# Reordering the end of a gated cross-attention and feed-forward kernel: who casts the last pair but one, and where its last addition stands

## The chip, the cores and the metric

The kernel runs on one core of one Trainium2 chip. The metric is the device time of one execution in microseconds (us), as the median over several timed runs. A profiled execution is a separate run of the same program with the hardware profiler on. A core has five engines that work side by side, each through its own list of instructions in order: TensorE (PE in the profile; PEld is its weight load), VectorE (DVE), ScalarE (ACT), GpSimd (POOL) and SyncE (SP), which issues DMAs.

## The reference

There are 16 sequences of 224 tokens with 512 features (3584 tokens) and, for each, 750 context rows with 384 features under a mask. Cut to what matters:

```python
def act_quant(x):
    scale = 127.0 / clip(max(abs(x), axis=-1), 1e-05)
    return clip(round(x * scale), -128, 127) / scale

def bitlinear(x, w, b):                 # w is rounded to -1, 0, 1 times a scale
    return act_quant(rmsnorm(x)) @ weight_quant(w).T + b

x = x + tanh(g_xattn) * cross_attention(layernorm(x), context, mask)   # 8 heads of 64
h = bitlinear(layernorm(x), w1, b1)     # 512 -> 2048
h = gelu(h)
x = x + tanh(g_ffn) * bitlinear(h, w2, b2)   # 2048 -> 512
```

The rounding of `act_quant` needs the greatest absolute value of a whole row first. So in the feed-forward part each row of `h` is finished, its maximum is taken, the row is scaled and rounded, transposed, and only then multiplied by `w2`.

## The kernel before, in words

The tokens are cut into 28 tiles of 128 rows; two tiles are a *pair*, 14 pairs, numbered 0 to 13, and a tile is row 0 or row 1 of its pair. "Row 12/1" below is the second tile of pair 12. The attention of one sequence after another runs on all engines, and the feed-forward work of the pairs is woven into it (`merge`). The changed lines belong to the end, where attention is over and only pairs 11, 12 and 13 are left.

What one row goes through in the feed-forward part:

- `project` multiplies the attention output by `wo` (TensorE, L1252) and VectorE adds it to the residual `y` (L1255). `normalise` makes the quantised `xq` of it on VectorE (L1290 to L1300) and, on POOL, the factor `c1`. The last pair's `xq` is transposed by TensorE in `turn_rows` (L1321) and copied out by ScalarE (L1322).
- `up`, or `up_last` for pair 13, multiplies by `w1` (L1333, L1411); VectorE evicts the product to `h` (L1341, L1419), ScalarE applies gelu (L1366, L1758, L1422). The last pair is evicted in halves; its rows live in the tiles named `h_last` (row 0) and `xoT` (row 1).
- The maximum of the row on VectorE: `a`, L1369, in `gelu`; for pair 13 the maxima of the halves, `am`, L1423, in `up_last`, and their combination, L1434, in `gelu_last`.
- The quantiser on VectorE (L1264, L1265), the rounding to 16-bit integers (L1372; L1441 for pair 13) and the cast of the integers to bf16, in place, in the tile `hq`. VectorE casts at L1375 for all pairs up to 11 and at L1442 for pair 13. For pair 12 ScalarE casts, in two halves, at L1379.
- The transposition of `hq` into `hqT`: by a DMA that SP issues (L1382), or, for rows 12/1, 13/0 and 13/1, in `turn_by_tensor` by TensorE (L1354) with ScalarE's copies (L1355).
- `down` multiplies by `w2`: 16 products into one accumulator (L1472). `down` can run something between its eighth and ninth product.
- `mean_square` sums squares on ScalarE (L1451), and POOL makes the factor `c2` in `measure_last` or `gelu` (L1272 to L1274).
- `store` adds the product, times `c2`, to `y` on VectorE (L1485), and POOL issues the indirect DMA that scatters the rows to the output (L1487).

The order of instructions on each engine is not the program's order: a scheduler lays out each engine's list before the run. `tc.issue_after(x)` tells it that what is written inside must stand behind `x`; an engine then works through its list strictly in turn, so an instruction that waits holds up all behind it. `late["rounded"]` remembers the last cast of a row by VectorE, and the end uses it as such an anchor. The end of the program, from the last up products on, reads before the change:

```python
    mean_square(i, 1)
    added, sent = store(i - 1, 1)
    gelu_last(i, 0)
    with tc.issue_after(added):
        gelu_last(i, 1)
```

Here i is 13: row 12/1 is added and sent, and both roundings of the last pair follow.

Of the kernel before, what the change touches and what calls it, by code (L numbers as in the profile page):

```python
# [11 lines left out]
ALU = mybir.AluOpType  # L12
AX = mybir.AxisListType
# [157 lines left out]
def flamingo_gated_kernel(  # L171
# [74 lines left out]

    stages = []
    compact = compact_path(ctx, tc, sh, x, context, out, late_loads, stages)
    next(compact)
    n_odd = nc.values_load(sh.n_odd[0:1, 0:1], min_val=0, max_val=2 * x.shape[0])  # L250
# [484 lines left out]
def compact_path(ctx, tc, sh, x, context, out, late_loads, stages):  # L735
# [3 lines left out]
    nc = tc.nc  # L739
# [3 lines left out]
    FF = sh.FF  # L743
# [12 lines left out]
    I16 = mybir.dt.int16  # L756
# [29 lines left out]
    def wide(shape, dtype, name):  # L786
        return ps_sim.tile(shape, dtype, tag="sim", name=name)
# [6 lines left out]
    def pow_half(dst):  # L794
        nc.gpsimd.tensor_tensor(dst, dst, sh.mhalf[:, : dst.shape[1]], ALU.pow)

    def small(name, n=2):
        return pa.tile([P, n], F32, tag=f"s{n}", name=name, bufs=24 if n == 2 else 6)


    def token(t):
        return sh.token[:, t // 7, t % 7 : t % 7 + 1]
# [433 lines left out]
    late = {}  # L1236
# [25 lines left out]
    def quantiser(amax, part, least, name):  # L1262
        k = small(f"k_{name}")
        nc.vector.tensor_scalar(k[:, part], amax[:, part], least, 1.0 / 127.0, ALU.max, ALU.mult)  # L1264
        nc.vector.reciprocal(k[:, part], k[:, part])  # L1265
        load["v"] += 300
        return k

    def unquantiser(amax, r, part, isw, name):

        c = small(f"c_{name}")
        nc.gpsimd.tensor_tensor(c[:, part], amax[:, part], r[:, part], ALU.mult)  # L1272
        nc.gpsimd.tensor_scalar(c[:, part], c[:, part], 1e-5, None, ALU.max)
        latest["p"] = nc.gpsimd.tensor_scalar(c[:, part], c[:, part], isw, None, ALU.mult).ins  # L1274
        return c
# [82 lines left out]
    def gelu(i, ks=(0, 1)):  # L1358
        f = pairs[i]
        name = f"{i}_{ks[0]}"  # L1360
        part = slice(ks[0], ks[-1] + 1)
        ss = small(f"ss_{name}")
        amax = small(f"a2_{name}")
        for k in ks:
            if (i, k) != (NPAIR - 2, 1):
                nc.scalar.activation(f["h", k], f["h", k], AF.Gelu)  # L1366
        for k in ks:
            h = f["h", k]
            nc.vector.tensor_reduce(amax[:, k : k + 1], h, AX.X, ALU.max, apply_absolute_value=True)  # L1369
            scale = quantiser(amax, slice(k, k + 1), 1e-5 * EPS**0.5, f"2_{i}_{k}")  # L1370
            hq = late["rows"].tile([P, FF], BF16, tag="hq", name=f"hq_{i}_{k}", bufs=3)
            nc.vector.tensor_scalar(hq.bitcast(I16), h, scale[:, k : k + 1], None, ALU.mult)  # L1372
            f["hqT", k] = hqT = late["rows"].tile([P, NF, P], BF16, tag="hqT", name=f"hqT_{i}_{k}", bufs=2)
            if i < NPAIR - 2:
                late["rounded"] = nc.vector.tensor_copy(hq, hq.bitcast(I16)).ins  # L1375
            else:
                for g in range(2):
                    cols = slice(g * FF // 2, (g + 1) * FF // 2)
                    nc.scalar.copy(hq[:, cols], hq.bitcast(I16)[:, cols])  # L1379
            f["hq", k] = hq  # L1380
            if (i, k) != (NPAIR - 2, 1):
                nc.sync.dma_start_transpose(out=hqT, in_=hq)  # L1382
        if (i, ks[0]) == (NPAIR - 2, 1):
            f["a2", 1] = amax[:, 1:2]
            return
        for k in ks:
            nc.scalar.activation(f["h", k], f["h", k], AF.Square, accum_out=ss[:, k : k + 1])  # L1387
        r = small(f"r2_{name}")
        nc.gpsimd.tensor_scalar(r[:, part], ss[:, part], 1.0 / FF, EPS, ALU.mult, ALU.add)
        pow_half(r[:, part])  # L1390
        c = unquantiser(amax, r, part, sh.isw[1], f"2_{name}")
        for k in ks:
            f["c2", k] = c[:, k : k + 1]
        load["v"] += len(ks) * (2282 + 1280 + 690)
        load["s"] += len(ks) * 2 * 1910 + 2600

    def up_last(i, k):

        f = pairs[i]
        if k == 0:  # L1400
            place = pa.tile([P, 12, S], F32, tag="pT", name="h_last", bufs=1)
            h = place.rearrange("p n q -> p (n q)")[:, :FF]
        else:
            h = xoT.rearrange("p n q -> p (n q)")[:, :FF]
        most = small(f"am_{i}_{k}")
        for g in range(2):
            ph = wide([P, 2, NB], F32, f"hp_{i}_{k}_{g}")
            for n in range(2):
                at = (2 * g + n) * NB
                for d in range(ND):  # L1410
                    last = nc.tensor.matmul(  # L1411
                        ph[:, n, :],
                        lhsT=f["xqT"][:, k * ND + d, :],
                        rhs=w1T[:, d, at : at + NB],
                        start=(d == 0),
                        stop=(d == ND - 1),
                    )
            cols = slice(2 * g * NB, 2 * (g + 1) * NB)
            nc.vector.scalar_tensor_tensor(  # L1419
                h[:, cols], ph.rearrange("t i n -> t (i n)"), f["c1", k], sh.b1[:, cols], ALU.mult, ALU.add  # L1420
            )
            nc.scalar.activation(h[:, cols], h[:, cols], AF.Gelu)  # L1422
            nc.vector.tensor_reduce(most[:, g : g + 1], h[:, cols], AX.X, ALU.max, apply_absolute_value=True)  # L1423
        f["h", k], f["most", k] = h, most
        return last.ins

    def gelu_last(i, k):

        f = pairs[i]
        name = f"{i}_{k}"  # L1430
        part = slice(k, k + 1)
        h = f["h", k]
        amax = small(f"a2_{name}")
        nc.vector.tensor_reduce(amax[:, part], f["most", k], AX.X, ALU.max)  # L1434
        scale = quantiser(amax, part, 1e-5 * EPS**0.5, f"2_{name}")
        hq = late["rows"].tile([P, FF], BF16, tag="hq", name=f"hq_{name}", bufs=3)
        f["hqT", k] = hqT = late["rows"].tile([P, NF, P], BF16, tag="hqT", name=f"hqT_{name}", bufs=2)
        half = FF // 2
        for g in range(2):
            cols = slice(g * half, (g + 1) * half)  # L1440
            nc.vector.tensor_scalar(hq.bitcast(I16)[:, cols], h[:, cols], scale[:, part], None, ALU.mult)  # L1441
            nc.vector.tensor_copy(hq[:, cols], hq.bitcast(I16)[:, cols])  # L1442
        f["hq", k], f["a2", k] = hq, amax[:, part]

    def mean_square(i, k):
        f = pairs[i]
        name = f"{i}_{k}"
        squares = small(f"sq_{name}")
        for g in range(2):
            junk = pa.tile([P, 2, D], F32, tag="x", name=f"sq_{name}_{g}", bufs=3)  # L1450
            nc.scalar.activation(  # L1451
                junk.rearrange("p k d -> p (k d)"),
                f["h", k][:, 2 * g * NB : 2 * (g + 1) * NB],
                AF.Square,
                accum_out=squares[:, g : g + 1],
            )
        f["r2", k] = r = small(f"r2_{name}")
        nc.gpsimd.tensor_tensor(r[:, 0:1], squares[:, 0:1], squares[:, 1:2], ALU.add)
        nc.gpsimd.tensor_scalar(r[:, 0:1], r[:, 0:1], 1.0 / FF, EPS, ALU.mult, ALU.add)
        pow_half(r[:, 0:1])  # L1460
# [20 lines left out]
    def store(i, k):  # L1481
        f = pairs[i]
        po = f["po", k]
        y = f["y"][:, k, :]
        added = nc.vector.scalar_tensor_tensor(y, po, f["c2", k], y, ALU.mult, ALU.add)  # L1485
        load["v"] += 700
        sent = nc.gpsimd.indirect_dma_start(  # L1487
            out=out_rows,
            out_offset=bass.IndirectOffsetOnAxis(ap=token(2 * i + k), axis=0),
            in_=y,  # L1490
            in_offset=None,
            bounds_check=B * S - 1,
            oob_is_err=False,
        )
        return added.ins, sent.ins

    NPAIR = NTOK // 2

    def up_pieces(i):
        p = []  # L1500
        for k in range(2):
            p += [(1.8, lambda g=g, k=k: up(i, k, g)) for g in range(2)]
            p.append((0.0, lambda k=k: gelu(i, (k,))))
        return p
# [244 lines left out]
    i = NPAIR - 1  # L1749
# [22 lines left out]
    with tc.issue_after(lowered):  # L1772
        up_last(i, 0)
        mean_square(i, 0)
        turn_rows(i, 1)
        raised = up_last(i, 1)
# [2 lines left out]
        turn_by_tensor(i - 1, 1)  # L1779
        lowered = down(i - 1, 1)  # L1780
    mean_square(i, 1)
    added, sent = store(i - 1, 1)
    gelu_last(i, 0)
    with tc.issue_after(added):
        gelu_last(i, 1)
    with tc.issue_after(raised):
# [44 lines left out]
```

## Time and profile before

| | us |
|---|---|
| timed runs, median of 3 (lowest to highest) | 740.0 (739.37 to 740.6) |
| profiled execution, its own time | 735.04 |
| profiled execution, span of the trace | 733.0 |
| TensorE busy in the span | 676.0 (92%) |
| VectorE busy | 492.2 (67%) |
| ScalarE busy | 416.2 (57%) |
| GpSimd busy | 394.1 (54%) |

The span is what the trace covers; 2 us of the profiled execution lie around it. The engines' shares are averages over the whole run. The granted TensorE clock was 0.981 of full speed over the span. A row of a timeline gives start, length, engine, line of the code, operation, output and inputs by name, shapes, how many instructions were merged, and in brackets how long the engine had been idle before it and what released it.

### The profile page before, as it was taken

How to read it: one execution, taken by the hardware profiler on the slowest of the kernel's cores; microseconds unless marked ns; L12 is line 12 of the kernel's file. 1: busy time of each engine (PE TensorE's matmuls, PEld its weight loads, DVE VectorE, ACT ScalarE, POOL GpSimd, SP SyncE). 2: the span in 40 equal slices, each digit the busy share in tenths (PEclk: the TensorE clock that was granted, in tenths of full speed). 3: DMA queues.
4: the chain of work that ended last, by engine and by line, in shares of the span. 5: the costliest groups of instructions: out<-in, count | busy, mean ns of one | idle time of the engine just before them, and what ended most of it. 6: DMA issues, size and time to landing. Idle time of an engine off the chain costs nothing.

```text
span 733.0 us, 11422 instructions
## 1 busy us (share of the span) xinstructions
PE 676.0 (92%) x3917; PEld 432.1 (59%) x3917; DVE 492.2 (67%) x1294; ACT 416.2 (57%) x978; POOL 394.1 (54%) x549
## 2 busy tenths in 40 slices
PE   4998899999999999897999999999999999999862
PEld 3876677666555656564556665766665665544331
DVE  5586856877484775673667857839585765889760
ACT  2549555384673864646627549547373746574560
POOL 5583676464464644755447562656545453554631
PEclk9989999999999999999999999999999999999997
DMA  7884031032222232321233321123313221422200
GB/s 236 288 288 144 14 104 32 16 75 57 65 54 58 83 58 72 70 59 58 54 61 104 58 81 38 41 72 74 83 43 72 58 59 44 86 73 58 58 15 33
DMA packets 79858, 56.74 MB, mean 77 GB/s; under 512 B 68176, under 2 KB 68320, under 8 KB 79664
## 3 DMA queue, kind: packets, MB, share of 16 engines
q1 hardware_dynamic: 71728, 30.17, 17.6%
q0 software_dynamic: 8064, 25.76, 11.4%
q8 instruction: 33, 0.54, 0.3%
q14 instruction: 33, 0.27, 0.1%
HBM read 32.06 MB, written 7.34 MB: 54 GB/s over the span
## 4 chain that ended last, share of the span: by engine, by line
PE 63%; DVE 10%; issue 9%; POOL 9%; ACT 4%; DMA 3%; POOLq 0%; DVEq 0%; ACTq 0%
PE qp L1066 11%; PE op L1252 10%; PE fp L1472 8%; PE hp L1333 8%; PE kp L946 5%; PE sim L1106 4%; PE vp L962 4%; PE ptp L1163 3%; PE av L1188 2%; POOL p L1140 2%; DVE a L1369 2%; PE xnp L1045 2%; POOL x L808 2%; DMA hqT<-hq 1%; POOL out_dram L1487 1%
## 5 line engine op out<-in xcount | busy, mean ns | idle before, releaser
L1140 POOL TENSOR_TENSOR p<-p,rec 112x768 f32<-112x768 f32 (+2 forms) x64 | 79.6, 1246 | 72.0 <-DVE rec L1139 28.1
L1130 ACT ACTIVATE p<-p,nm 112x192 f32<-112x192 f32 (+2 forms) x256 | 104.8, 413 | 10.3 <-DVE nm L1120 7.3
L1472 PE MATMUL fp<-w2T,hqT 128*128 128x512 fp8e4 x448 | 102.6, 382 | 3.8 <-DMA hqT<-hq 2.2
L1066 PE MATMUL qp<-xnT,wq_sb 128*128 128x224 f32 x512 | 105.1, 359 | 0.6 <-ACT xnT L781 0.6
L1252 PE MATMUL op<-wo_sb,xoT 128*128 128x512 f32 x224 | 103.7, 599 | 0.0
L1333 PE MATMUL hp<-w1T,xqT 128*128 128x512 fp8e4 x416 | 99.3, 383 | 3.0 <-DVE nm L1120 1.4
L1066 PEld LDWEIGHTS qp<-xnT,wq_sb 128*128 128x128 f32 x512 | 97.0, 193 | 6.4 <-issue 3.1
L1341 DVE SCALAR_TENSOR_TENSOR h<-hp,c,b_bc 128x1024 f32<-128x1024 f32 x52 | 66.5, 1281 | 43.6 <-PE hp L1333 43.3
L1120 DVE CUSTOM_DVE_ANT_0 p<-sim,mask 112x192 f32<-112x192 f32 (+2 forms) x224 | 56.0, 303 | 32.5 <-PE sim L1106 31.9
L1472 PEld LDWEIGHTS <-hqT 128*128 128x128 bf16 x448 | 42.7, 98 | 58.8 <-issue 6.3
L1369 DVE TENSOR_REDUCE a<-h 128x1 f32<-128x2048 f32 x26 | 59.3, 2281 | 20.3 <-ACT h L1366 20.3
L1487 POOL DMA_INDIRECT out_dram<-y,token x28 | 32.0, 1143 | 67.2 <-DVE y L1485 62.1
L1333 PEld LDWEIGHTS <-xqT 128*128 128x128 bf16 x416 | 39.9, 98 | 47.4 <-issue 8.5
L1485 DVE SCALAR_TENSOR_TENSOR y<-fp,c,y 128x512 f32<-128x512 f32 x28 | 20.9, 746 | 68.0 <-PE fp L1472 66.4
L1252 PEld LDWEIGHTS op<-wo_sb,xoT 128*128 128x128 f32 x224 | 40.7, 190 | 38.8 <-issue 36.3
L946 PE MATMUL kp<-ctxT,wk_sb 128*128 128x192 f32 (+1 forms) x360 | 59.9, 316 | 0.0
L946 PEld LDWEIGHTS kp<-ctxT,wk_sb 128*128 128x128 f32 x360 | 54.5, 198 | 5.4 <-issue 3.8
L1387 ACT ACTIVATE h<-h 128x2048 f32<-128x2048 f32 x25 | 47.7, 1909 | 17.1 <-DVE hq L1372 11.8
L1312 POOL TENSOR_TENSOR y<-y,b_bc 128x512 f32<-128x512 f32 x28 | 37.0, 1321 | 34.6 <-DVE fx L1292 34.3
L781 ACT COPY pT<-ptp 128x448 f32<-128x448 f32 (+1 forms) x62 | 32.3, 536 | 39.9 <-PE ptp L1163 39.7
L781 ACT COPY qT<-qp 128x448 f32<-128x448 f32 x29 | 15.4, 532 | 65.7 <-PE qp L1066 65.4
L1106 PE MATMUL sim<-kT,qT 64*112 64x192 f32 (+2 forms) x512 | 50.8, 311 | 0.6 <-DVE nm L1120 0.6
(200 smaller groups left out, 1250.5 us busy)
## 6 DMA issues: line engine op xcount, KB each, us to landing
raw<-in_L_ffn_w_dram SPq DMA_DIRECT2D x16, 512.0 KB, 5.4
wq_sb<-in_L_xattn_W_q_dram SPq DMA_DIRECT2D x1, 1024.0 KB, 5.8
b_bc<-in_L_ffn_b_dram SPq DMA_DIRECT2D x1, 1024.0 KB, 8.3
wk_sb<-in_L_xattn_W_k_dram SPq DMA_DIRECT2D x1, 768.0 KB, 7.4
wv_sb<-in_L_xattn_W_v_dram SPq DMA_DIRECT2D x1, 768.0 KB, 8.8
wo_sb<-in_L_xattn_W_o_dram SPq DMA_DIRECT2D x1, 512.0 KB, 4.0
wo_sb<-in_L_xattn_W_o_dram SPq DMA_DIRECT2D x2, 256.0 KB, 6.0
y<-in_x_dram,token POOLq DMA_INDIRECT x28, 3.5
```

Source lines behind the costliest of these rows:

```text
L946: nc.tensor.matmul(pk[:, p - p0, :], lhsT=sh.wk[:, c, p * P : (p + 1) * P], rhs=st["ctxT"][:, c, :cap], start=(c == 0), stop=(c == NC - 1),)
L1066: nc.tensor.matmul(pq[:, i, :], lhsT=sh.wq[:, d, (p + i) * P : (p + i + 1) * P], rhs=st["xnT"][:, d, :], start=(d == 0), stop=(d == ND - 1),)
L1106: nc.tensor.matmul(sim[:, j, i, :cap], lhsT=st["qT"][j * DH : (j + 1) * DH, p, q * TQ : (q + 1) * TQ], rhs=keys["kT"][j * DH : (j + 1) * D ...
L1120: nc.vector.tensor_tensor_reduce(out=probs[:, h, :cap], in0=sim[:, j, i, :cap], in1=keys["mask"][:, first + j * begin : first + j * begin ...
L1130: nc.scalar.activation(probs[:, h, :cap], probs[:, h, :cap], AF.Exp, bias=nmax, scale=-1.0, accum_out=total[:TQ, h : h + 1],)
L1140: nc.gpsimd.tensor_tensor(probs[:, :, first : first + cap], probs[:, :, :cap], rec[:TQ].unsqueeze(2).to_broadcast([TQ, 4, cap]), ALU.mult,)
L1252: last = nc.tensor.matmul(po, lhsT=xoT[:, d, at : at + P], rhs=sh.wo[:, d, :], start=(d == 0), stop=(d == ND - 1))
L1333: last = nc.tensor.matmul(ph[:, n, :], lhsT=f["xqT"][:, k * ND + d, :], rhs=w1T[:, d, at : at + NB], start=(d == 0), stop=(d == ND - 1),)
L1341: nc.vector.scalar_tensor_tensor(h[:, cols], ph.rearrange("t i n -> t (i n)"), f["c1", k], sh.b1[:, cols], ALU.mult, ALU.add)
L1369: nc.vector.tensor_reduce(amax[:, k : k + 1], h, AX.X, ALU.max, apply_absolute_value=True)
L1387: nc.scalar.activation(f["h", k], f["h", k], AF.Square, accum_out=ss[:, k : k + 1])
L1472: last = nc.tensor.matmul(po, lhsT=f["hqT", k][:, n, :], rhs=w2T[:, n, :], start=(n == 0), stop=(n == NF - 1))
```

## The change

Three things are changed, all at the end. First, `gelu` casts every row on VectorE, pair 12 included, and remembers that cast as `late["rounded"]`. Second, in `up_last` the maxima of the last pair are laid behind that anchor, so the rounding and cast of row 12/1 stand in front of them on VectorE. Third, `gelu_last` returns its last cast, and `store` of row 12/1, its addition on VectorE and its scatter on POOL, is laid behind the casts of row 13/0; the rounding of row 13/1 stays behind the addition.

```diff
@@ gelu
-            if i < NPAIR - 2:
-                late["rounded"] = nc.vector.tensor_copy(hq, hq.bitcast(I16)).ins
-            else:
-                for g in range(2):
-                    cols = slice(g * FF // 2, (g + 1) * FF // 2)
-                    nc.scalar.copy(hq[:, cols], hq.bitcast(I16)[:, cols])
+            late["rounded"] = nc.vector.tensor_copy(hq, hq.bitcast(I16)).ins
             f["hq", k] = hq
@@ up_last
             nc.scalar.activation(h[:, cols], h[:, cols], AF.Gelu)
-            nc.vector.tensor_reduce(most[:, g : g + 1], h[:, cols], AX.X, ALU.max, apply_absolute_value=True)
+            with tc.issue_after(late["rounded"]):
+                nc.vector.tensor_reduce(most[:, g : g + 1], h[:, cols], AX.X, ALU.max, apply_absolute_value=True)
@@ gelu_last
             nc.vector.tensor_scalar(hq.bitcast(I16)[:, cols], h[:, cols], scale[:, part], None, ALU.mult)
-            nc.vector.tensor_copy(hq[:, cols], hq.bitcast(I16)[:, cols])
+            rounded = nc.vector.tensor_copy(hq[:, cols], hq.bitcast(I16)[:, cols])
         f["hq", k], f["a2", k] = hq, amax[:, part]
+        return rounded.ins
@@ the end
     mean_square(i, 1)
-    added, sent = store(i - 1, 1)
-    gelu_last(i, 0)
+    with tc.issue_after(gelu_last(i, 0)):
+        added, sent = store(i - 1, 1)
     with tc.issue_after(added):
         gelu_last(i, 1)
```

In the compiled order other instructions move with these. On VectorE row 13/0's reduction, scale and rounding stand ahead of row 13/1's residual addition, and the first maximum of the last pair stands behind the eviction of row 13/1's first half instead of before it. On ScalarE the gelu of row 13/1's first half stands ahead of the squares of row 13/0. On TensorE the four transposes of row 13/0's `xq` stand between the eighth and ninth product of row 12/0 instead of behind the sixteenth. On POOL one small operation trades places with its neighbour. SP's list is the same. The lines of the changed kernel after L1374 are 3 to 5 lower than those before.

## The prediction

> **What bounds the kernel now.** The busy shares come first and settle little: TensorE is busy 92% of the 733.0 us span, but the change touches only the last 60 us, so that stretch has to be read by itself. I read, in this order, the chain of waits from 640 us on, the timelines of VectorE and TensorE over the same stretch, then windows of it, and the rows of the casts.
>
> The chain (start, length, what it went through):
>
> ```profile
> 678.55 1.04 ACT hq L1379
> 679.59 0.03 ACT h L1387
> 679.61 4.57 DMA hqT<-hq
> 684.18 0.05 issue
> 684.23 3.64 PE fp L1472 x16
> ...
> 701.51 3.77 PE fp L1472 x16
> 705.28 0.03 issue
> 705.31 0.02 DVEq L1485
> 705.33 0.04 issue
> 705.37 0.75 DVE y L1485
> ```
>
> Read two things. ScalarE's second half-cast of pair 12, row 0 ends at 679.59; the transposing DMA then takes 4.57 us, and the products of that row start at 684.23, though the projection before them ended at 683.14. And later VectorE's addition y of pair 12, row 1 starts as the 16 products of that row end. After this the chain goes through POOL's small c operations to 711.24 and then shows 5.59 us of "issue"; nothing ran on POOL there, so I follow VectorE and TensorE instead (start, length, operation, in brackets the idle time before):
>
> ```profile
> 702.45 1.22 DVE L1423 TENSOR_REDUCE am<-xoT 128x1 f32<-128x1024 f32 x1 [0.63 <-ACT xoT L1422]
> 705.37 0.75 DVE L1485 SCALAR_TENSOR_TENSOR y<-fp,c,y 128x512 f32<-128x512 f32 x1 [1.71 <-PE fp L1472]
> 706.61 1.42 DVE L1441 TENSOR_SCALAR hq<-h_last,k 128x1024 int16<-128x1024 f32 x2
> 707.94 0.96 DVE L1442 CAST hq<-hq 128x1024 bf16<-128x1024 int16 x2
> ```
>
> ```profile
> 708.63 1.48 PE L1354 MATMUL hqp<-ident,hq 128*128 128x128 bf16 x16 [3.36 <-DVE hq L1442]
> 710.36 2.95 PE L1472 MATMUL fp<-w2T,hqT 128*128 128x512 fp8e4 x8 [0.25 <-ACT hqT L1355]
> 713.15 1.06 PE L1354 MATMUL hqp<-ident,hq 128*128 128x128 bf16 x16
> 714.04 5.34 PE L1472 MATMUL fp<-w2T,hqT 128*128 128x512 fp8e4 x24
> ```
>
> The last maximum ends at 703.67. The last pair's rounding needs nothing more, yet it starts at 706.61: VectorE first waits 1.71 us for the addition's products and then adds. TensorE idles 3.36 us meanwhile, and its next 8 products take 2.95 us where 16 took 3.75. The windows say why (window, its length, busy time of PE, PEld, DVE, ACT, POOL, then the granted TensorE clock, DMA share, GB/s):
>
> ```profile
> 81.02:84.43 3.41, 1.24 (x13) 1.03 (x14) 3.41 (x11) 1.26 (x5) 3.12 (x5) 1.00 0.00 0
> 695.40:698.80 3.40, 1.65 (x10) 0.58 (x8) 3.40 (x4) 3.40 (x7) 0.82 (x3) 1.00 0.00 0
> 705.66:709.07 3.41, 0.44 (x8) 0.45 (x9) 3.34 (x12) 0.00 (x0) 2.88 (x7) 1.00 0.05 18
> 709.07:712.49 3.42, 3.17 (x18) 1.53 (x16) 2.02 (x4) 1.93 (x2) 2.10 (x4) 0.51 0.17 63
> ```
>
> After a nearly empty window TensorE ran at half clock for 3.4 us. So the end is a ring of VectorE, ScalarE and TensorE in which VectorE's order decides.
>
> **The change part by part.** Times below are of the profiled execution (735.04 us, span 733.0); the timed runs have a median of 740.0 (739.37 to 740.6), 5.0 above it. I work out a difference at the end and take it off 740.0, as nothing before 677 us is changed. All places are from the compiled order of both kernels.
>
> *Step 1, row 0's cast.* Removed: two ScalarE casts (2 x 1.03 us). Added: one VectorE cast, 0.69 us, behind the addition that ends at 677.94, so done at 678.56 instead of 679.59. SP issues the same transposing DMA 1.03 earlier; with 4.57 us it lands at 683.15, when the projection (end 683.14) frees TensorE. Products start at 683.2, gain 1.0. ScalarE, 2 us freer, does its squares earlier, with slack on POOL.
>
> *Step 2, the normalisation of pair 13.* Its row 0 now goes ahead of row 1 on VectorE: reduction, scale and rounding end at 683.6, row 1's residual addition (ready at 683.14) at 684.25, row 0's cast at 684.45 instead of 687.05. So TensorE's four transposes (0.39) now stand in the middle of the 16 products (3.63), which end at 687.25; the up products follow at once (688.76 before). Row 1's chain on VectorE by its own rows (0.68, 0.18, 0.48, 0.67, 0.3, 0.48), the addition y (0.75, ready at 687.3) and the cast end at 688.45 instead of 689.91.
>
> *Step 3, VectorE is full here* (8.00 of 8.00 us in 690 to 698), so each operation counts. From 688.4: a2 of row 12/1 2.28, two h_last evictions 2 x 1.27, rounding 1.27, end 694.5; first xoT eviction to 695.7 (about 699.2 before, because one maximum, 1.2, now comes later); the moved cast 0.69 to 696.3 (ScalarE's ended at 699.61); two maxima to 698.6; second xoT eviction to 699.8; a third maximum to 701.0.
>
> *Step 4, ScalarE.* Its order is now: gelu of the first xoT half (until 696.8, it waits for the eviction at 695.7), squares 2.1 (698.85), two hqT copies (700.75; their transposes end at 697.6), gelu of the second half (701.75). Queued behind that early gelu are the squares and the copies, so TensorE's products of row 12/1 run from 699.95 to 703.7 (705.26 before). The last maximum starts at 701.8 and ends at 703.0 instead of 703.67. Six microseconds of ScalarE work stand between the first xoT eviction and this maximum, which is why 3.5 us gained there shrink to 0.65.
>
> *Step 5, the moved addition.* The rounding follows the maximum directly: with the 0.57 us of small operations it starts at 703.55 instead of 706.61, gain 3.06; without steps 1 to 4 the order alone would give 2.4 (idle 1.71 plus the addition's 0.7). Row 0's transposes start at 705.6 (708.63), its products at 707.3 (710.36). The addition now follows row 0's casts, 705.75 to 706.45, then row 1's scale (0.5) and rounding: casts end at 709.0 instead of 711.1. POOL's scatter of that row waits for the addition (until 706.45, before 706.12), and its c operations wait behind the scatter: they end near 711.5 instead of 711.24. The next addition needs its c only at 712, so that costs nothing; the cover is 0.5 to 1 us.
>
> *Step 6, the clock.* Before, 8 products ran at half clock, 2.95 us for 1.82: 1.1 us. After, TensorE's gap is about 1.9 us. The trace's row: windows with 0.44 and 1.24 us of TensorE work of 3.41 were followed by half clock, one with 1.65 was not. The Trainium skill ("TensorE: Matmul & The Clock Gate", What's actually happening) has the clock drop after an idle window of about 3.4 us; a gap of 1.9 us would then be free and the gain 3.06 + 1.1 = 4.2. By the rows, windows over the new gap, with the transposes, hold 1.3 to 1.9 us, at the edge, and the phase is unknown; if it drops, the gain is about 3.0. A half-clock stretch on the products from 699.95 would end them near 705.4, still ahead of 705.6. I take 0.6 of the 1.1, nearer to neither row.
>
> *Step 7, contention.* A rule speaks against the cast on VectorE: "SBUF — State Buffer", Who interferes with whom, has casts contend with GpSimd, where "Whoever issues first gets the shared pair for the whole instruction". The casts' rows:
>
> ```profile
> L1375 DVE CAST hq<-hq x24: 653/688/3275, 159.6 to 667.1; 128x2048 bf16<-128x2048 int16 x24
> 206.57 3.27 DVE L1375 CAST hq<-hq 128x2048 bf16<-128x2048 int16 x1
> ```
>
> One of 24 lost 2.6 us, with POOL's row operations (206.54 to 209.29) on top of it. At the new places POOL has a scatter's issue (678.23 to 679.33) and, at 695.7, nothing. By the rule a cast that loses to the scatter ends near 680 and step 1 is void; by the row of a rounding that overlapped such an issue (204.98, 1.39 us for 1.28) it costs 0.1. I take the row.
>
> Sum: 3.06 + 0.6 = 3.7 us, so 736.3.
>
> **The rivals.** *A, the early half brings nothing.* The transpose lands no earlier (it now starts beside the scatter of row 11/1, which already overlaps it) or a cast stalls; then the two casts' 1.4 us on the full VectorE eat steps 1 to 4, and step 5's 2.4 with little clock is left: about 737.5. For: landings of these DMAs range from 4.2 to 6.0 us. Against: the median is 4.3.
>
> *B, one long stall.* One of the two casts loses 2.6 us to POOL as at 206.57: 3.7 - 2.6, 738.9, within what can't be told from no change.
>
> *C, slower: both casts stall behind POOL.* Place: 677.9 and 695.7 on VectorE, with everything of the last pair queued behind. Price 2 x 2.6 = 5.2 against 3.7: 741.5. It decides once the stalls on the chain pass 3.7 us, and slower can be measured past 5.2. For: the one row. Against: POOL's timeline has no row operation at either place.
>
> *D, the order does not act as said*, or another wait takes the place of the addition's (the last maximum still held by ScalarE until after 704): 740. Against: the compiled order has the addition behind the roundings.
>
> **How the numbers follow.** This measurement can tell about 0.2%, 1.5 us, from no change. Main forecast 0.72: 736.3, by itself 735.2 to 737.2. A 0.13: 737.5. B 0.07: 738.9. C 0.05: 741.5. D 0.03: 740. Faster is the first and A, 0.85; same is B and D, 0.10; slower is C, 0.05. The range 735.1 to 738.5 takes in the first two with the clock's both ends (4.2 and 3.0) and some of the error in a chain of thirty estimated steps.
>
> **What would show it.** Right: products of row 12/0 start within 0.2 us of the projection's end; xqp transposes in the middle of them; first xoT eviction about 3.5 us earlier; last maximum only 0.3 to 1 us earlier; no idle before the rounding of the last pair, and its transposes about 3 us earlier; 8 products in 1.8 or 2.95 us tell step 6. Wrong: a cast of 128x2048 well over 0.7 us in the last 60 us; an idle gap ahead of the last maximum of more than 2 us on ScalarE's gelu; an addition y of the last pair that waits for POOL's c.

## The result, and the profile after

The changed kernel takes 736.91 us (median of 7 runs, 733.75 to 738.65) where the kernel before takes 740.6 beside it: ratio 0.9939, 95% interval 0.9915 to 0.9963. (The medians are 3.7 us apart, the means, 736.23 and 740.76, 4.5; the ratio goes with the means.) Two later comparisons of the same pair gave 0.9925 (0.9903 to 0.9946) and 0.9941 (0.9917 to 0.9964). So it is faster, by about what was forecast (736.3). But step 1 of the sum went the other way and carried the steps behind it along: nearly all that can be shown of the gain is step 5's.

Every execution reaches the end with an offset of its own: the projection of pair 13, ahead of which nothing was changed, starts at 676.11 us before, at 679.72 after, and between 676.7 and 681.6 in the other traces. That spread is larger than the effect. So places are given below as **offsets from the start of that projection** (L1252): a row's start, or its start plus its length, minus the start of the first row here. The last addition ends at offset 44.13 before and 42.57 after. The rows before, then after:

```profile
676.11 7.03 PE L1252 MATMUL op<-wo_sb,xoT 128*128 128x512 f32 x16
684.23 3.63 PE L1472 MATMUL fp<-w2T,hqT 128*128 128x512 fp8e4 x16 [1.09 <-DMA hqT<-hq]
...
719.49 0.75 DVE L1485 SCALAR_TENSOR_TENSOR y<-fp,c,y 128x512 f32<-128x512 f32 x1 [2.71 <-PE fp L1472]
```

```profile
679.72 7.03 PE L1252 MATMUL op<-wo_sb,xoT 128*128 128x512 f32 x16
...
721.54 0.75 DVE L1482 SCALAR_TENSOR_TENSOR y<-fp,c,y 128x512 f32<-128x512 f32 x1 [2.70 <-PE fp L1469]
```

VectorE's timeline of the changed kernel:

```profile
681.47 0.68 DVE L1374 CAST hq<-hq 128x2048 bf16<-128x2048 int16 x1
...
701.11 0.68 DVE L1374 CAST hq<-hq 128x2048 bf16<-128x2048 int16 x1
...
707.16 1.22 DVE L1419 TENSOR_REDUCE am<-xoT 128x1 f32<-128x1024 f32 x1 [0.79 <-ACT xoT L1417]
...
708.86 1.42 DVE L1437 TENSOR_SCALAR hq<-h_last,k 128x1024 int16<-128x1024 f32 x2
...
712.02 0.75 DVE L1482 SCALAR_TENSOR_TENSOR y<-fp,c,y 128x512 f32<-128x512 f32 x1 [1.07 <-PE fp L1469]
```

Both moved casts (L1374) take 0.68 us. The rounding of row 13/0 follows the last maximum after 0.48 us of small operations (2.94 before, with the addition between), and the addition y now stands behind it. But the maximum itself ends at 708.38, offset 28.66, where it ended at 27.56 before: 1.1 us later. TensorE's timeline says why:

```profile
689.06 1.90 PE L1469 MATMUL fp<-w2T,hqT 128*128 128x512 fp8e4 x8 [2.31 <-DMA hqT<-hq]
690.80 0.39 PE L1321 MATMUL xqp<-ident,xq 128*128 128x128 bf16 x4
...
705.32 6.59 PE L1469 MATMUL fp<-w2T,hqT 128*128 128x512 fp8e4 x16 [2.40 <-ACT hqT L1355]
711.75 1.06 PE L1354 MATMUL hqp<-ident,hq 128*128 128x128 bf16 x16
713.46 1.90 PE L1469 MATMUL fp<-w2T,hqT 128*128 128x512 fp8e4 x8 [0.66 <-ACT hqT L1355]
```

The products of row 12/0 wait 2.31 us for their transposing DMA (1.09 before). Those of row 12/1 wait 2.40 us for ScalarE's copies and then take 6.59 us for 16 where full clock needs 3.63. The chain of waits shows both:

```profile
682.22 6.80 DMA hqT<-hq
689.01 0.05 issue
689.06 1.90 PE fp L1469 x8
...
702.19 2.17 ACT sq L1448 x4
704.37 0.90 ACT hqT L1355
705.27 0.05 issue
705.32 6.61 PE fp L1469 x16
711.97 0.04 issue
712.02 0.75 DVE y L1482
```

The DMA took 6.80 us where it took 4.57 before, and two squares on ScalarE (four instructions, each square with the read of its sum) stand in front of the copies. Three windows around the 16 products (columns as before: PE busy first, granted clock after POOL):

```profile
701.31:704.73 3.42, 1.07 (x16) 0.90 (x16) 3.42 (x4) 3.42 (x6) 0.20 (x2) 0.97 0.00 0
704.73:708.14 3.41, 2.82 (x7) 1.01 (x8) 2.62 (x3) 3.41 (x6) 0.76 (x2) 0.50 0.00 0
708.14:711.56 3.42, 3.42 (x10) 1.20 (x9) 2.70 (x8) 1.06 (x3) 1.56 (x3) 0.53 0.00 0
```

The window with TensorE's gap has 1.07 us of work; half clock follows for two windows. It falls on row 12/1's products instead of the last pair's first eight, which are back at 1.90 us for 8 (2.95 before).

### The profile page after: what moved, and what is told of

The parts are those of the page before. It is cut to its first block, busy times and chain, and to the rows that moved or that the text cites. A ratio compares the mean times of both kernels' runs of the same rounds, so it can differ in the third digit from the quotient of the medians.

```text
span 735.1 us, 11419 instructions
## 1 busy us (share of the span) xinstructions
PE 678.2 (92%) x3917; PEld 433.7 (59%) x3917; DVE 490.1 (67%) x1296; ACT 413.0 (56%) x974; POOL 395.3 (54%) x549
## 4 chain that ended last, share of the span: by engine, by line
PE 58%; issue 11%; POOL 10%; DVE 8%; DMA 5%; ACT 3%; POOLq 0%; SPq 0%; ACTq 0%; DVEq 0%
PE op L1252 11%; PE qp L1066 9%; PE fp L1469 8%; PE hp L1333 8%; PE sim L1106 4%; PE kp L946 4%; PE vp L962 4%; PE ptp L1163 2%; DMA hqT<-hq 2%; DMA raw<-in_L_ffn_w_dram 2%; PE av L1188 2%; POOL p L1140 2%; POOL out_dram L1484 1%; DVE a L1369 1%; POOL x L808 1%
## 5 line engine op out<-in xcount | busy, mean ns | idle before, releaser
L1469 PE MATMUL fp<-w2T,hqT 128*128 128x512 fp8e4 x448 | 104.6, 387 | 6.5 <-DMA hqT<-hq 3.4
L1252 PE MATMUL op<-wo_sb,xoT 128*128 128x512 f32 x224 | 103.7, 599 | 0.0
L1252 PEld LDWEIGHTS op<-wo_sb,xoT 128*128 128x128 f32 x224 | 40.7, 190 | 38.8 <-issue 36.4
```

The source lines that it names most:

```text
L1252: last = nc.tensor.matmul(po, lhsT=xoT[:, d, at : at + P], rhs=sh.wo[:, d, :], start=(d == 0), stop=(d == ND - 1))
L1469: last = nc.tensor.matmul(po, lhsT=f["hqT", k][:, n, :], rhs=w2T[:, n, :], start=(n == 0), stop=(n == NF - 1))
```

## The experiments

All in one table. Ratios are timed, against the kernel before on the same chip. The other columns come from the one trace of each kernel: the wait in front of the products of row 12/0, then offsets from the projection's start, then the time from the last pair's first rounding to the end.

| kernel | ratio (95%) | wait 12/0 | last maximum ends | rounding starts | end | rounding to end |
|---|---|---|---|---|---|---|
| before | 1 | 1.09 | 27.56 | 30.50 | 44.13 | 13.63 |
| after | 0.9939 (0.9915–0.9963) | 2.31 | 28.66 | 29.14 | 42.57 | 13.43 |
| a2_after_again | 0.9925 (0.9903–0.9946) | 2.23 | 28.58 | 29.06 | 41.43 | 12.37 |
| a3_after_beside | 0.9941 (0.9917–0.9964) | 2.40 | 28.75 | 29.23 | 41.60 | 12.37 |
| e1_add_only | 0.9933 (0.9908–0.9958) | 1.08 | 27.55 | 28.04 | 42.31 | 14.27 |
| e2_add_back | 1.0025 (1.0013–1.0036) | 2.34 | 28.69 | 32.27 | 46.32 | 14.05 |
| e3_row0_scalar | 0.9941 (0.9924–0.9959) | 1.10 | 28.21 | 28.70 | 41.06 | 12.36 |
| e4_scatter_later | 0.9943 (0.9919–0.9966) | 0 | 27.49 | 27.97 | 40.33 | 12.36 |
| e4b (e4 again) | 0.9939 (0.9917–0.9961) | 0 | 27.51 | 28.00 | 40.36 | 12.36 |
| e5_squares_later | 0.9934 (0.9914–0.9955) | 2.27 | 27.81 | 28.30 | 42.31 | 14.01 |
| e6_busy | 0.9936 (0.9916–0.9957) | 2.38 | 30.23 | 30.71 | 43.07 | 12.36 |
| e7_both | 0.9927 (0.9903–0.9950) | 0 | 26.71 | 27.19 | 42.02 | 14.83 |
| e8_both_busy | 0.9919 (0.9888–0.9949) | 0 | 26.71 | 27.19 | 39.55 | 12.36 |
| e8b (e8 again) | 0.9921 (0.9892–0.9950) | 0 | 26.71 | 27.19 | 39.55 | 12.36 |

Read the last column first. From the last pair's rounding to the end it is 12.36 us in every trace in which no half-clock stretch slows this part, and 1.1 to 2.5 more where one does. The rest is where the rounding starts.

The timed ratios do not follow the traces that finely: all kernels with the moved addition lie between 0.9919 and 0.9943 with intervals that overlap, while their traces end between 39.55 and 43.07 us. So timing shows the moved addition alone (e1 and e2); what the other experiments say rests on their traces, one or two of each.

**The addition alone, and everything but the addition.** e1 is the kernel before with only the third part of the change; e2 is the changed kernel with only that part undone.

```diff
# e1, on the kernel before (gelu_last returns its last cast)
-    added, sent = store(i - 1, 1)
-    gelu_last(i, 0)
+    with tc.issue_after(gelu_last(i, 0)):
+        added, sent = store(i - 1, 1)
# e2, on the changed kernel: the reverse
```

> The kernel before with the moved addition alone: row 12/1 is added and sent behind the casts of row 13/0; casts and maxima stand as before. Measure: the tail, from the first product of pair 13's projection to the end of the last addition y (44.1 us in the trace of before, 42.6 after the whole change). If the addition's wait was the dominant cost (theory 1), the rounding follows the last maximum and the tail is about 44.1 - 2.4 = 41.7, give or take 1 us of half clock; about 2 to 3 us off the timed median. If VectorE's order of casts and maxima made the gain (theory 2), the tail stays near 44.

> The changed kernel with the addition of row 12/1 put back in front of the rounding of row 13/0; casts by VectorE and the maxima's place kept. Theory 1: most of the gain is gone, tail 43.5 to 46 us depending on whether the half clock falls on row 12/1's products; timed within 0.3% of before. Theory 2: tail stays near 42.6 and about 3 us faster than before.

VectorE's timeline, e1 and then e2:

```profile
707.10 1.42 DVE L1441 TENSOR_SCALAR hq<-h_last,k 128x1024 int16<-128x1024 f32 x2
...
711.10 0.75 DVE L1486 SCALAR_TENSOR_TENSOR y<-fp,c,y 128x512 f32<-128x512 f32 x1 [1.92 <-PE fp L1473]
```

```profile
707.74 0.75 DVE L1482 SCALAR_TENSOR_TENSOR y<-fp,c,y 128x512 f32<-128x512 f32 x1 [2.35 <-PE fp L1469]
...
708.98 1.42 DVE L1437 TENSOR_SCALAR hq<-h_last,k 128x1024 int16<-128x1024 f32 x2
```

In e1 the last maximum stands where it stood (27.55) and the rounding is 2.46 us earlier (28.04 for 30.50); it is timed at 0.9933. In e2 the rounding again waits for the products and the addition, and the kernel is 0.25% slower than before, at the edge of what can be told. So the moved addition carries the gain. The early half alone gains nothing (e2), and beside the moved addition it adds nothing that can be told: 0.9939 with it, 0.9933 without (e1).

**Why row 12/0 came late.** In e3 ScalarE casts that row again; in e4 the addition and scatter of row 11/1 are laid behind row 13/0's residual addition, so that the scatter's issue moves off the place where the transposing DMA starts.

```diff
# e3, in gelu
-            late["rounded"] = nc.vector.tensor_copy(hq, hq.bitcast(I16)).ins
+            if (i, k) != (NPAIR - 2, 0):
+                late["rounded"] = nc.vector.tensor_copy(hq, hq.bitcast(I16)).ins
+            else:
+                for g in range(2):
+                    cols = slice(g * FF // 2, (g + 1) * FF // 2)
+                    nc.scalar.copy(hq[:, cols], hq.bitcast(I16)[:, cols])
# e4 (project remembers its residual addition as late["residual"])
-    store(i - 2, 1)
     ...
             projected = project(i, k)
+            if k == 0:
+                with tc.issue_after(late["residual"]):
+                    store(i - 2, 1)
```

> The changed kernel with row 12/0 cast by ScalarE in two halves as before; row 12/1 is still cast by VectorE and the addition still moved. In the trace of the change the transposing DMA of row 12/0, issued 0.4 us after POOL began to issue the scatter of row 11/1, took 6.8 us to the first product that needs it, 4.6 before. Collision theory: issued 1 us later, behind the scatter, it takes about 4.6 again, the products of row 12/0 start about 1 us after the projection's end instead of 2.3, and the tail is about 1.2 us shorter than 42.6. The prediction's theory: the early cast is worth 1 us, so the tail is 1 us longer than with it.

> The changed kernel with the addition and scatter of row 11/1 moved behind the residual addition of row 13/0 on VectorE, so that the transposing DMA of row 12/0 runs alone. Collision theory: it lands about 4.3 us after its issue, so the products of row 12/0 start as the projection ends, 2 us earlier than in the change's trace; tail about 40.5 us and about 2 us faster than the change. If the long landing has another cause (chance, or the early issue itself), it stays at 6 to 7 us and the tail near 42.6.

> The same kernel as e4_scatter_later, run beside e8_both_busy. Theory 1: the wait in front of the products of row 12/0 stays 0 to 0.2 us, since scatter and transposing DMA no longer overlap, and the end is 40.3 to 41.5 us by where the half clock falls; Theory 2 (the zero wait was luck of one execution): the wait is 1 us or more again. Timed ratio about 0.993.

TensorE's timeline, e3 and then e4 (no bracket: no wait):

```profile
685.76 3.63 PE L1474 MATMUL fp<-w2T,hqT 128*128 128x512 fp8e4 x16 [1.10 <-DMA hqT<-hq]
```

```profile
683.70 2.97 PE L1471 MATMUL fp<-w2T,hqT 128*128 128x512 fp8e4 x13
```

With ScalarE's later cast the wait is that of before. With the early cast and the scatter elsewhere it is gone, and it was gone again in e4b. (The cast ends 0.5 us earlier still in e4, as the addition of row 11/1 no longer stands in front of it.) Timed, e4 is no faster than the change, 0.9943 against 0.9939, where about 2 us had been expected. So in the traces the early cast as such works, but in the change its DMA starts at 682.22 in the middle of the scatter's issue on POOL (timeline of POOL, after):

```profile
681.84 1.28 POOL L1484 DMA_INDIRECT out_dram<-y,token  x1 [7.19 <-DVE y L1482]
```

In the five traces with that overlap and a readable landing (after, a2, e2, e5, e6) the DMA took 6.71 to 6.86 us; in before, e1 and e3, where it starts 0.28 us behind the end of the scatter's issue, 4.55 to 4.57; in e4, e4b and e8, with the scatter far off, 4.4 to 4.5. That an early start alone makes it slow is thus ruled out.

The packets of the two DMA queues show what happens, read in windows of 0.2 us. In the kernel before, the scatter's 80 packets move from 679.8 to 680.9 and the transposing DMA's behind them, until 683.5. In the changed kernel the transposing DMA's packets come first, from 683.3; from 684.7 the scatter's move among them, and both are done only at about 688.3. In e4 the transposing DMA's run alone, from 679.9 to 682.5. So the scatter's data was on its way at that time in the kernel before as well; what is new is that the two share the engines instead of following each other. Why the scatter's data comes 1.6 us behind the end of its issue in the changed kernel, and 0.5 us in the one before, was not tried, and an issue nearby does not always cost: in before, two other such DMAs had a scatter's issue begin 1.25 us after their start (321.59 and 372.80) and took 4.4 and 5.4 us, and one with no scatter's issue near (502.05) took 6.0.

**ScalarE's order.** e5 is the changed kernel with the squares of row 13/0 behind the copies of row 12/1 and behind the gelu of row 13/1's second half, so that neither waits for them. To keep VectorE's order, the maxima stand in a loop of their own in `up_last` (not in the cut below). e7 is e4 and e5 together.

```diff
         up_last(i, 0)
-        mean_square(i, 0)
     ...
-        turn_by_tensor(i - 1, 1)
+        turned = turn_by_tensor(i - 1, 1)
         lowered = down(i - 1, 1)
+    with tc.issue_after(late["gelu_last"]):
+        mean_square(i, 0)
     mean_square(i, 1)
```

> The changed kernel with one ScalarE order altered: the squares of row 13/0 stand behind the hqT copies of row 12/1 and the gelu of row 13/1's second half. Ring theory (the prediction's step 4: ScalarE work between the first xoT eviction and the last maximum eats the gain): row 12/1's products start about 1.8 us earlier after the first xoT eviction (4.1 us behind it in the change's trace, counted from the eviction's end), the last maximum 0.8 us earlier, the tail is 1 to 1.8 us shorter than the change's. If VectorE alone sets the last maximum, the tail is unchanged.

> The change with the scatter of row 11/1 later (as in the run where the transposing DMA ran alone, tail 40.3 us) and with the squares of row 13/0 later as well. If the two gains are independent, the tail is 39.5 us, 0.8 shorter than with the scatter alone, and the timed median is about 1% below before. If one hides the other, the tail stays at 40.3.

TensorE's timeline of e5:

```profile
705.36 3.63 PE L1471 MATMUL fp<-w2T,hqT 128*128 128x512 fp8e4 x16 [0.66 <-ACT hqT L1355]
711.66 1.07 PE L1354 MATMUL hqp<-ident,hq 128*128 128x128 bf16 x16 [2.67 <-DVE hq L1440]
713.39 3.54 PE L1471 MATMUL fp<-w2T,hqT 128*128 128x512 fp8e4 x8 [0.66 <-ACT hqT L1355]
```

The wait for the copies falls from 2.40 to 0.66 us, and the rounding starts 0.8 us earlier than after, as expected. But now TensorE idles 2.67 us in front of the last pair, and its first 8 products take 3.54 us: the half clock has moved onto the path, and nothing is left of the gain (end 42.31, after 41.43 to 42.57; 1 to 1.8 us less had been expected). e7 shows it more plainly: its rounding is as early as any, at 27.19, and its end is 42.02 where 39.5 had been expected. Windows of e7:

```profile
705.40:708.82 3.42, 1.14 (x6) 0.29 (x3) 3.32 (x8) 3.42 (x8) 0.91 (x2) 0.99 0.00 0
708.82:712.23 3.41, 2.77 (x19) 1.96 (x20) 3.31 (x9) 2.93 (x4) 2.83 (x6) 0.50 0.00 0
712.23:715.65 3.42, 3.42 (x17) 1.77 (x16) 0.69 (x2) 0.00 (x0) 1.64 (x7) 0.51 0.22 81
```

**Filling a gap.** e6 is the changed kernel with eight unread products in TensorE's gap in front of the products of row 12/1; e8 is e7 with eight in the gap behind them. Neither changes what is computed.

```diff
+    def keep_busy(i):
+        junk = wide([P, 2, NB], F32, "junk_products")
+        for n in range(8):
+            last = nc.tensor.matmul(
+                junk[:, 0, :], lhsT=pairs[i]["xqT"][:, 0, :], rhs=w1T[:, 0, :NB], start=True, stop=True
+            )
+        return last.ins
# e6, on the changed kernel
+        with tc.issue_after(late["last_turn"].ins):   # the last transpose of row 12/1
+            busy = keep_busy(i)
+        with tc.issue_after(busy):
+            lowered = down(i - 1, 1)
# e8, on e7
         lowered = down(i - 1, 1)
+    with tc.issue_after(lowered):
+        raised = keep_busy(i)
```

> The changed kernel with 8 products added whose result nobody reads, in TensorE's gap of 2.4 us between the transposes of row 12/1 and its products. Clock theory: no nearly empty window is left there, the products of row 12/1 take about 3.75 us instead of 6.6 at half clock, they end before the casts of row 13/0, and the tail is about 1.1 us shorter than 42.6. If the half clock does not depend on TensorE's own work, they take 5 to 6.6 us again and the tail stays.

> e7_both with eight products whose result nobody reads (pair 13's xqT by w1T) put on TensorE behind the products of pair 12, row 1; the output's arithmetic is unchanged. In e7_both TensorE idled 2.67 us there, and the transposes and the first 8 products of the last pair then ran at half clock (1.89 and 3.60 us where 1.06 and 1.90 are full). Theory 1 (the gap in front of the last transposes is what puts the half clock on them, and the half clock is what gave the earlier gains back): the transposes take 1.06, the 8 products 1.90, and the end, counted from the start of pair 13's projection to the end of the last addition, falls from 42.02 to about 39.5 us. Theory 2 (a half-clock stretch comes once in this end wherever it is, as in the run that filled the earlier gap): it falls on other products, ahead of or behind these, and the end is 40.5 or more. The timed ratio would be about 0.990 by the first and 0.993 by the second.

> The same kernel as e8_both_busy, now on one chip with the changed kernel as it stands. Theory 1 (the end of e8_both_busy, 39.55 us from the start of pair 13's projection to the last addition, is its own and no luck of the clock's phase): again 39.4 to 40 us, transposes and products of the last pair at full clock, and a timed median 2 to 3 us below that of the changed kernel beside it. Theory 2 (the phase decides anew): a half-clock stretch falls on the last pair's products and the end is 41 us or more.

The changed kernel itself was run twice more, beside e5 to e7 and beside e8b:

> The changed kernel itself once more, on the same chip as the three that follow and with a second trace. The transposing DMA's late landing should be there again (products of row 12/0 start 2.3 us after the projection's end). Where the half clock falls may differ: tail 42.6 us if row 12/1's products take 6.6 us again, about 41.5 if they take 5.3 or less. Timed 0.5 to 0.6% faster than before.

> The changed kernel itself, beside e8b_again on one chip: an end of 41.4 to 42.6 us by where the half clock falls, as in its two earlier traces, and a timed ratio to the kernel before of about 0.993.

TensorE's timeline, e6 and then e8:

```profile
687.18 3.39 PE L1477 MATMUL fp<-w2T,hqT 128*128 128x512 fp8e4 x8 [2.38 <-DMA hqT<-hq]
...
702.36 1.89 PE L1361 MATMUL junk_products<-w1T,xqT 128*128 128x512 fp8e4 x8
704.92 3.63 PE L1477 MATMUL fp<-w2T,hqT 128*128 128x512 fp8e4 x16 [0.67 <-ACT hqT L1355]
```

```profile
701.07 3.63 PE L1481 MATMUL fp<-w2T,hqT 128*128 128x512 fp8e4 x16 [0.66 <-ACT hqT L1357]
704.54 1.89 PE L1363 MATMUL junk_products<-w1T,xqT 128*128 128x512 fp8e4 x8
707.37 1.07 PE L1356 MATMUL hqp<-ident,hq 128*128 128x128 bf16 x16 [0.94 <-DVE hq L1450]
709.09 1.90 PE L1481 MATMUL fp<-w2T,hqT 128*128 128x512 fp8e4 x8 [0.66 <-ACT hqT L1357]
```

e6 did not decide what it was made for: the products of row 12/1 ran at full clock behind the filler, but in that execution the half clock had already fallen at 686.89, behind the wait for row 12/0's DMA, and cost about 1.5 us there. e8 did, by the traces: the rounding stays at 27.19 as in e7, transposes and products of the last pair run at full clock, and the end falls from 42.02 to 39.55, in both of its traces; 39.5 was expected. Beside each other on one chip, e8 took 732.58 us (7 runs, 731.5 to 736.31) and the changed kernel 734.53 (8 runs, 733.65 to 736.94): 1.95 us between the medians, 2.05 between the ends in their traces. That is the best version here, though the two ranges overlap and the gain is little more than the 0.2% that can be told. Against e7 the timing shows no gain: 0.9919 and 0.9921 (0.990 expected) stand beside e7's 0.9927, within each other's intervals.

## Why the prediction was right, and where it was not

**Step 5, the addition: right, and nearly all of it.** The order alone was put at 2.4 us; e1 shows 2.46. POOL's c's were indeed covered: the last two additions of the changed kernel wait for TensorE, 2.75 and 2.70 us, not for POOL.

**Step 1, row 12/0 a microsecond earlier: wrong.** Its products start at offset 9.34 instead of 8.12, 1.2 us later. The cast did finish earlier relative to the rest, at 2.43 where ScalarE's ended at 3.48; the failed term is the 4.57 us of the DMA, taken over from before although the start moved under the scatter of row 11/1. It measured 6.80. This is what rival A named as a possibility and the forecast took at 0.13. e4 shows what step 1 is worth without the scatter: no wait in front of the products.

**Step 2, the normalisation ahead: right on VectorE, late on TensorE.** Row 13/0's cast ends at 8.35 where the forecast's 684.45 is 8.34. The transposes stand in the middle of the products and the up products follow at once, but these are shifted by the late row and start at 13.03 where 11.14 was forecast.

**Steps 3 and 4, the last maximum 0.65 us earlier: wrong in sign, by step 1's fault.** It is 1.1 later. The lengths were right: from the end of the first xoT eviction to the end of the last maximum the forecast has 7.3 us, the trace 7.19, squares and copies queued behind the early gelu as said. But that eviction ends at 21.47 where 19.59 was forecast, because VectorE's full stretch begins behind the late row 12/0, at 14.16 where 12.29 was forecast. By the forecast's own figures the new order gives back 2.85 of the 3.5 us gained at the eviction; only 1.6 was gained, too little to pay for it. The table agrees: with row 12/0 where it was before, casts, maxima and ScalarE's order alone put the last maximum 0.66 later (e3 against e1, 28.21 and 27.55); row 12/0's cast with its late DMA adds 0.45 (after against e3). e4, without the late DMA, has the rounding at 27.97, and e7, with the squares moved too, at 27.19; the forecast's 703.55 is 27.44. For the same reason row 12/1's products start at 25.60 where 23.84 was forecast.

**Step 6, the clock: between, with the gap in another place.** I took 0.6 of 1.1. From the rounding to the end the three traces of the changed kernel gain 0.20, 1.26 and 1.26 us. The gap of about 1.9 us that I put in front of the last pair's transposes is not there in any of them (0.20 us in a2, none in the others): the late products of row 12/1 fill it. The gap is the 2.40 us in front of those products, and the half clock fell on them in all three. I had allowed for one window there. In the first trace it lasted two: the products ended only at 32.19 and held back y and the next transposes, which start at 32.03, 0.5 us earlier than before, where 3 was forecast.

**Step 7, contention: right.** The two casts took 0.68 us each, the row's value, so rivals B and C did not come. The first overlapped a scatter's issue on POOL, and it was the issue that took longer, 1.28 us where the same one took 1.10 before. The Trainium skill ("SBUF — State Buffer", Who interferes with whom) has whoever issues first hold the port pair that VectorE's casts and GpSimd share. The cast began first, so by it the issue would lose up to 0.31 us (681.84 to 682.15). The direction fits, but the transposing DMA's own issue on SP, from 682.22, overlaps it as well, and no run here separates the two. Rival D did not come: the order acted as compiled.

**Signs and luck.** Of the signs that were to show the prediction right, these came: the transposes in the middle of the products, the rounding without idle time before it and the 8 products in 1.90 us. These did not: row 12/0's start (2.31 us behind the projection), the xoT eviction (1.6 us earlier, not 3.5), the last maximum (1.1 us later) and the last pair's transposes. By mechanism this is rival A, an early half that brings nothing and a step 5 that does. Its price was 737.5, and 736.91 lies midway between that and 736.3. Step 1 missed and took steps 2 to 4 along, and something outside the sum made up for them (below), so that the medians are 3.7 us apart, just as forecast, is luck.

**What stays open.** By the traces the end is 1.6, 2.7 and 2.5 us shorter than before (42.57, 41.43 and 41.60 against 44.13); the timed medians differ by 3.7, 5.3 and 3.8. There is one trace of the kernel before, a short execution (735.04 us where the timed median is 740.0), and its half clock may have fallen better than usual, or the spread ahead of the end differs between the programs. For e8 both ways agree better: 4.6 by trace, 4.6 and 5.7 timed. So 1.3 to 2.6 us of the timed gain lie outside what the traces of the end show, and they made up for steps 1, 3 and 4; what they are is open.

## What to carry to other kernels

When a step starts a DMA earlier, don't carry its old duration over: look at what is issued at the new time, on POOL's queue as well, and whose data will then share the engines. An engine that runs its list in order can swallow an early start whole: ask what stands in the list between the thing that now comes first and the one the others wait for. Near an end with gaps on TensorE, a gain that moves a gap in front of the last products can be paid back in clock; filling that one gap with unread products took 2.5 us off the end in the traces here, though not in the timed ratios. And a total that comes out right does not confirm its terms: take the sum apart on one time base, as with the offsets here, before trusting it.

## What was not expected of the hardware

Half-clock stretches came in whole windows of 3.41 us, and one window was not always the end of it. Windows in which TensorE worked 0.44 (before), 1.07 (after), 1.14 (e7), 1.24 (e1), 1.29 (e4) and 1.31 us (e6) were followed by half clock; one with 1.65 (before) was not. At half clock, windows with 2.54 (e1), 2.77 (e7) and 2.82 us (after) of work were followed by a second one; windows with 3.12 (e6), 3.17 (before) and 3.41 (e4) were not. (The windows' edges are read to 0.2 us.) The Trainium skill ("TensorE: Matmul & The Clock Gate", What's actually happening) has the clock fall after an idle window and rise after a busy one; these rows put numbers on idle and busy: the one lies between 1.31 and 1.65 us of 3.41, the other between 2.82 and 3.12. In a3 a window with 1.42 us (718.23 to 721.65) kept full clock for the next, so the first is rather near 1.4. TensorE need not be idle for a whole window, then: gaps of 0.83 and 2.40 us around the transposes of row 12/1 were enough in all three traces of the changed kernel.

A transposing DMA that starts under a scatter's issue took 6.80 us (4.57 before), the packets of both moving at once.
